# Block outputs of a fused two-layer kernel: four full-array products, or eight products of 64 rows and 64 columns

## The chip, the core and the metric

The kernel runs on one core of a Trainium2 chip. A core has TensorE (matrix products, results in PSUM), VectorE (DVE), ScalarE (ACT), GpSimd (POOL) and SyncE (SP, which issues the transfers here). PSUM has eight banks of 2 KiB for each of 128 partitions; a bank holds 512 f32 numbers. The metric is the time of one execution on the device in microseconds (us), the median of several runs. Lower is better.

## What is computed

x has the shape (4, 64, 256, 256), f32. Two layers follow each other, each a residual around a group norm.

```
x = x + L0(group_norm(x))     # 1x1 convolutions, a 3x3 depthwise one, an 8x8 FFT filter, a GELU gate
x = x + L1(group_norm(x))     # two state-space blocks over the image, one by rows, one by columns
...
fx = layer_norm(seq)                       # over the 64 channels
h = s5_scan(fx)                            # forward and backward scan, 64 complex states
x = gelu(h) + fx
fx2 = layer_norm(x)                        # over the 64 channels
y = fx2 @ ff_enc.T @ ff_dec.T + fx2
...
out = concat(y_rows, y_columns) @ fusion_w.T + fusion_b
```

The change lies in the last three lines: layer 1, from gelu(h) + fx to its share of the fused output. ff_enc, ff_dec, the `+ fx2`, the centring of the second layer norm and fusion_w are multiplied together ahead of time into one matrix of 64 by 64 for each of the two directions.

## The kernel before

Layer 0 runs first, strip by strip of eight rows over the four images, and writes its result to a scratch tensor in DRAM (`x1d`). Then each image goes through layer 1 in a first pass (`pass_a`), a scan (`scan`) and a second pass (`pass_b`). The first pass normalises, stores the normalised strips (`fxd`) and makes one summary for each short segment of a sequence; the scan runs over the summaries; the second pass fills in the states within the segments and makes the output.

Partitions hold 64 channels twice: the lower 64 partitions are one row of the image, the upper 64 another row, with the same channels.

The second pass works in units. A unit is one strip of 16 rows (s, 16 of them) in one direction (d=1 by columns, d=0 by rows); the list `order` takes d=1, then d=0 of each strip, so 32 units an image and 128 in all. A unit has four blocks of 512 columns, taken in the order `blocks = (1, 2, 0, 3)`. Its steps, each a function in `pass_b`:

- `states` (L1378): products into PSUM tile `pst` (two banks, one buffer), then one VectorE operation for each step (tiles `stm`, `sto`). For d=1 these are products over 128 rows with 512 columns; for d=0 they are pairs of 64 rows and 256 columns, one half in each of the two banks.
- `filt` (L1409): products into `ph` (one bank, two buffers). For d=1 these use the whole array, 512 and 256 columns; for d=0 they write halves of 64 output partitions, two beside each other. GELU on ScalarE, an addition on GpSimd and a square on ScalarE follow, and give `xr` (the block's 128x512 result) and `sq`.
- `sums` (L1449) and `rstd_of` (L1463): sums over channels into `pv` (one bank), four transposes back into `pv`, and the reciprocal standard deviation `r` of every position, once a unit.
- `outputs` (L1478): for one block, four products with 128 columns of `xr` as the stationary operand (`lhsT`) and the matrix `wb[d][:, NB[d]]` as the moving one, into `px`. That matrix is 128 by 128 with the 64x64 matrix twice on its diagonal and zeros elsewhere. VectorE multiplies the result by `r` into `y` (positions on partitions).
- `emit` (L1488): four transposes of `y` into another `px`, which VectorE adds to the strip (`acc`, tile `strip`); after the last block of a d=0 unit the strip is stored.

`px` is one bank with three buffers, shared by `outputs` and `emit`. With `pst` 2, `ph` 2, `px` 3 and `pv` 1 all eight banks are taken.

The order on every engine is the order of the program: `mm` and `vec` keep it. The loop over n runs four quarters for each unit. In a quarter come, one after the other: `states` of the unit ahead (first part), the steps of earlier units that are due in the first half, `filt` (first part), `states` (second part), `filt` (second part), and the steps due in the second half. The table `behind` says what is due:

```
for i, k in enumerate(blocks):
    behind[7 + i, 1] = [(outputs, k)]
    behind[8 + i, 0] = [(emit, k)]
behind[4, 1] = [(sums,)]
behind[5, 1] = [(rstd_of,)]
```

The first number is 4 times the delay in units plus the quarter, the second is the half. So every quarter ends with the `outputs` of one block; in the first quarter `sums` of the unit before comes right behind them, in the second `rstd_of`. The next quarter's `states` follows, and then the block's `emit`. After the last unit of an image three more rounds of the loop hold only these late steps.

A product over f32 appears in the trace as two weight loads and two matmuls. In the profile, the form `64*128 64x256` means 64 rows by 128 columns of the array and a moving operand of 64 by 256; `128*64` means all rows and 64 columns of the array.

Of the kernel before, what the change touches and what calls it, by code (L numbers as in the profile page):

```python
# [16 lines left out]
C = 64  # L17
HID = 170
S = 256
P = 128  # L20
# [90 lines left out]
def tile_kernel(ctx: ExitStack, tc: tile.TileContext, x, cst, w0, winp, wdwp, w1, out):  # L111
# [3 lines left out]
    def new(pool, shape, tag, bufs=None, dt=F32):  # L115
        return pool.tile(shape, dt, tag=tag, name=tag, **({} if bufs is None else {"bufs": bufs}))
# [77 lines left out]
    with ExitStack() as l0:  # L194
# [17 lines left out]
        for h in range(2):  # L212
            p = slice(h * C, (h + 1) * C)
# [39 lines left out]
        with tc.tile_pool(name="pssp", bufs=1, space=PSUM) as pp:  # L253
            ps = new(pp, [P, 512], "sp")
# [6 lines left out]
        NA, NB = (16, 8), (32, 25)  # L261
# [16 lines left out]
        with ExitStack() as l1w:  # L278
# [35 lines left out]
            def tmp(n=2, dt=F32):  # L314
                n_tmp[0] += 1
                return new(sp, [P, n], f"tmp{n_tmp[0]}", None, dt)
# [49 lines left out]
            def mul(a, b):  # L366
                o = tmp()
                TT(o, a, b, ALU.mult)
                return o
# [28 lines left out]
            t = mul(lim, lim)  # L398
            TT(den, den, t, ALU.add)
            vec.reciprocal(di, den)  # L400
            qr, qi, u, t = tmp(), tmp(), mul(lbi, lim), mul(nr, lre)
            TT(qr, t, u, ALU.add)
            u, t = mul(nr, lim), mul(lbi, lre)
# [142 lines left out]
            u, t, r, i = mul(ur, ur), mul(ui, ui), tmp(), tmp()  # L546
# [9 lines left out]
            n = 1  # L556
# [26 lines left out]
            for d in range(2):  # L583
                w = lambda name, d=d: wts[d][:, W1_AT[name][0] : W1_AT[name][0] + W1_AT[name][1]]
                ps = new(pw, [P, 512], "pw")
# [9 lines left out]
            for d in range(2):  # L595
                ps = new(pw, [P, 512], "pw")
# [7 lines left out]
                for h in range(2):  # L604
                    p = slice(h * C, (h + 1) * C)
                    TS(wos[d][p, p], mts[d][p, 0, :], par(d, "g2")[p], None, ALU.mult)
            burst[1]()
            for d in range(2):
                mm(
                    psb[:, 0:1], lhsT=mts[d][0:C].rearrange("p h c -> p (h c)"), rhs=par(d, "b2")[0:C],  # L610
                    start=(d == 0), stop=(d == 1),
                )
                ps = new(pw, [P, 512], "pw")
# [14 lines left out]
        pp = l0.enter_context(tc.tile_pool(name="ps0", bufs=2, space=PSUM))  # L628
# [321 lines left out]
        for b in range(nb):  # L950
            if b + 1 < nb:
                nxt_stats = new(wk, [P, 2 * NS0, 6], "stats1")
            for s in range(NS0):
                n = b * NS0 + s
# [97 lines left out]
    def rows_of(s):  # L1052

        for k in range(2):
            for hi in range(2):
                yield slice(k * C, (k + 1) * C), slice(4 * hi, 4 * hi + 4), s * R1 + 8 * hi + (k ^ hi)
# [22 lines left out]
    with tc.tile_pool(name="psn", bufs=2, space=PSUM) as pn:  # L1079
        for b in range(nb):  # L1080
# [4 lines left out]
            ps = new(pn, [P, 512], "pn")  # L1085
# [227 lines left out]
    def pass_b(b):  # L1313

        with ExitStack() as es:
# [4 lines left out]
            wb = [new(wp, [P, NB[d] + 1, P], f"wb{d}") for d in range(2)]  # L1320
# [20 lines left out]
            pp = es.enter_context(tc.tile_pool(name="psb", bufs=2, space=PSUM))  # L1341
# [7 lines left out]
            def mm(*args, **kw):  # L1349
                tc.keep_in_program_order(nc.tensor.matmul(*args, **kw))  # L1350
# [127 lines left out]
            def outputs(u, i):  # L1478


                ps, xr = new(pp, [P, 512], "px", 3), u.pop(("xr", i))
                for k in range(4):
                    mm(ps[:, k * P : (k + 1) * P], lhsT=xr[:, k * P : (k + 1) * P], rhs=wb[u["d"]][:, NB[u["d"]]], start=True, stop=True)
                y = u["y", i] = new(wk, [P, 512], "y")
                yv, pv = (t.rearrange("p (k h c) -> p k h c", k=4, h=2) for t in (y, ps))
                vec.tensor_tensor(yv, pv, u["r"][:, :, i].unsqueeze(3).to_broadcast([P, 4, 2, C]), ALU.mult)

            def emit(u, i):  # L1488
                y, acc = u.pop(("y", i)), u["acc"]
                ps = new(pp, [P, 512], "px", 3)  # L1490
                for k in range(4):
                    tc.keep_in_program_order(nc.tensor.transpose(ps[:, k * P : (k + 1) * P], y[:, k * P : (k + 1) * P], ident))  # L1492
                if u["d"] == 1:
                    o = acc[:, 2 * i : 2 * i + 2].rearrange("p r (g q) -> p r q g", q=16)
                    vec.tensor_tensor(o, ps.rearrange("p (r q g) -> p r q g", r=2, q=16), o, ALU.add)
                    return
                o = acc.rearrange("p r (g q) -> p q (r g)", q=16)[:, 4 * i : 4 * i + 4]
                vec.scalar_tensor_tensor(o, ps.rearrange("p (q t) -> p q t", q=4), bias, o, ALU.add, ALU.add)
                if i == blocks[-1]:
                    for h, r, row in rows_of(u["s"]):  # L1500
                        nc.sync.dma_start(out=out[b, :, row : row + 7 : 2, :], in_=acc[h, r])
# [3 lines left out]
            blocks = (1, 2, 0, 3)  # L1505
            behind = {}
# [3 lines that stand above are left out]
# [7 lines left out]
            for n in range(len(order) + 3):  # L1517
                if n < len(order):
                    s, d = order[n]
# [110 lines left out]
```

## Time and profile before

| | |
|---|---|
| median of 3 runs | 8972.83 us (8968.28 to 8975.56) |
| the profiled execution | 8968.82 us |
| its span, first to last instruction | 8967.0 us |
| granted TensorE clock over the span | 0.986 |
| TensorE busy, weight loads busy | 8424.2 us, 5727.6 us |
| VectorE busy | 7092.5 us |
| outputs: matmuls into px from wb, xr | 4096, 569.5 us busy |
| outputs: y on VectorE | 512, 354.1 us busy, 692 ns each |
| emit: transposes into px | 2048, 325.6 us busy |
| emit: additions to the strip on VectorE | 256 of 1025 ns, 256 of 1117 ns |

PE is TensorE's matmul row, PEld its weight loads, which can run beside matmuls. A group line gives the source line, engine, operation, tiles (out<-in), form, count, then busy us, mean ns of one, and the idle time of the engine before them with what ended it. A timeline line gives the start in us, the duration in us, the engine, the operation and how many instructions are merged in it. The ends of matmul rows are modelled; their starts are not.

### The profile page before, as it was taken

The page shows a single profiled execution, that of the slowest core. Times are in us where ns is not written, and L with a number is a line of the kernel's source. Part 1 is how long each engine was busy: PE and PEld are TensorE (multiplying, and loading weights), DVE is VectorE, ACT ScalarE, POOL GpSimd, SP SyncE. Part 2 cuts the span into 40 slices and gives each one's busy share as a digit, 9 for nine tenths or more (in the row PEclk, how much of TensorE's full clock was granted, in tenths as well). Part 3 has the DMA queues.
Part 4 walks back from the last instruction along what each step waited for, and adds up shares of the span by engine and source line. Part 5 has one row for each costly group of instructions (what it writes and reads, how often), then busy time and mean ns, then how long its engine had stood idle before and what let it go on. Part 6 is the DMA issues. An engine that isn't in the chain of part 4 may idle for free. (4 is left out here: it accounts for less than half of the span.)

```text
span 8967.0 us, 184750 instructions
## 1 busy us (share of the span) xinstructions
PE 8424.2 (94%) x79478; PEld 5727.6 (64%) x79478; DVE 7092.5 (79%) x8837; ACT 3404.5 (38%) x5094; POOL 2408.0 (27%) x1282
## 2 busy tenths in 40 slices
PE   3999999999999999998899988999988999889999
PEld 2666666666666666665466655566654666555666
DVE  7999999999999999995767756777656677567776
ACT  3444444444444444436322245222263222452222
POOL 3000000000000000005644446444356444464443
PEclk9999999999999999999999999999999999999999
DMA  7444344444444333325233345133352333451332
GB/s 176 101 104 102 95 108 100 105 101 97 102 104 103 83 87 83 87 63 175 103 81 81 90 120 178 49 84 82 82 169 103 81 81 90 120 178 49 84 82 70
DMA packets 655264, 904.19 MB, mean 101 GB/s; under 512 B 43120, under 2 KB 584816, under 8 KB 618864
## 3 DMA queue, kind: packets, MB, share of 16 engines
q1 hardware_dynamic: 654448, 892.37, 37.3%
q8 instruction: 627, 10.27, 0.5%
q14 instruction: 189, 1.55, 0.1%
HBM read 583.86 MB, written 275.05 MB: 96 GB/s over the span
## 5 line engine op out<-in xcount | busy, mean ns | idle before, releaser
L207 PE MATMUL m<-v,sw 64*128 64x256 f32 (+1 forms) x8192 | 1541.8, 392 | 1.6 <-DVE v L303 1.1
L207 PEld LDWEIGHTS m<-v,sw 64*128 64x128 f32 (+1 forms) x8192 | 1121.7, 188 | 505.1 <-issue 359.2
L303 DVE SCALAR_TENSOR_TENSOR acc<-xat,taps,acc 128x1024 f32<-128x1024 f32 x1024 | 1311.5, 1281 | 16.6 <-ACT acc L164 2.9
L1445 POOL TENSOR_TENSOR xr<-xr,fx 128x512 f32<-128x512 f32 x512 | 650.6, 1271 | 1863.8 <-ACT xr L1444 1378.9
L1350 PE MATMUL pst<-fx,wb 64*128 64x256 f32 (+1 forms) x4992 | 1017.3, 438 | 37.5 <-DVE stm L303 18.3
L694 POOL MEMSET at<- 64x256 f32 x4 | 1.2, 308 | 3525.4 <-DVE v L303 3525.4
L1350 PEld LDWEIGHTS pst<-fx,wb 64*128 64x128 f32 (+1 forms) x4992 | 508.4, 187 | 372.1 <-issue 244.4
L1475 POOL TENSOR_TENSOR rs<-ve,mhalf 128x32 f32<-128x32 f32 x128 | 695.3, 5432 | 99.2 <-DVE ve L303 99.2
L303 DVE SCALAR_TENSOR_TENSOR stm<-stm,step,pst 128x512 f32<-128x512 f32 x640 | 478.6, 748 | 232.9 <-PE pst L1350 219.3
L1446 ACT ACTIVATE sq<-xr 128x512 f32<-128x512 f32 x512 | 322.8, 631 | 872.5 <-POOL xr L1445 872.5
L207 PEld LDWEIGHTS m<-ct,hw 128*64 128x64 f32 x16384 | 509.7, 138 | 117.7 <-issue 117.7
L303 DVE SCALAR_TENSOR_TENSOR sto<-sto,step,pst 128x512 f32<-128x512 f32 x512 | 382.9, 748 | 242.7 <-PE pst L1350 228.8
L1350 PE MATMUL px<-wb,xr 128*128 128x128 f32 x4096 | 569.5, 282 | 0.0
L303 DVE TENSOR_TENSOR z<-xc,pr 128x512 f32<-128x512 f32 x256 | 264.8, 1036 | 385.2 <-PE pr L1106 382.2
L1350 PEld LDWEIGHTS px<-wb,xr 128*128 128x128 f32 x4096 | 519.8, 193 | 54.2 <-issue 41.8
L303 DVE TENSOR_TENSOR y<-px,rs 128x512 f32<-128x512 f32 x512 | 354.1, 692 | 229.2 <-PE px L1350 220.1
L1350 PE MATMUL ph<-sto,wb 128*64 128x128 f32 (+1 forms) x5120 | 528.0, 299 | 0.0
L207 PE MATMUL m<-ct,hw 128*64 128x64 f32 x16384 | 527.3, 223 | 0.0
L1350 PE MATMUL ph<-stm,wb 128*64 128x128 f32 (+1 forms) x5120 | 525.0, 299 | 0.0
L1350 PEld LDWEIGHTS ph<-stm,wb 128*64 128x64 f32 (+1 forms) x5120 | 409.0, 147 | 144.5 <-issue 128.0
L164 POOL TENSOR_TENSOR rs<-ve,mhalf 128x32 f32<-128x32 f32 x64 | 347.7, 5433 | 566.0 <-DVE ve L303 554.3
L1350 PEld LDWEIGHTS ph<-sto,wb 128*64 128x64 f32 (+1 forms) x5120 | 405.0, 147 | 143.0 <-issue 129.8
(316 smaller groups left out, 15615.0 us busy)
## 6 DMA issues: line engine op xcount, KB each, us to landing
strip<-x1d SPq DMA_DIRECT2D x512, 256.0 KB, 7.4
fx<-fxd SPq DMA_DIRECT2D x128, 1024.0 KB, 6.9
at<-in_x_dram SPq DMA_DIRECT2D x248, 320.0 KB, 4.5
sx<-in_x_dram SPq DMA_DIRECT2D x256, 256.0 KB, 4.0
pr<-in_x_dram SPq DMA_DIRECT2D x256, 256.0 KB, 4.2
er<-in_x_dram SPq DMA_DIRECT2D x256, 256.0 KB, 4.1
x1d<-x SPq DMA_DIRECT2D x256, 256.0 KB, 4.0
fxd<-fv SPq DMA_DIRECT2D x64, 1024.0 KB, 4.7
```

The lines of the kernel that those rows point to most:

```text
L164: return lambda *args, **kw: tc.keep_in_program_order(getattr(self.engine, name)(*args, **kw))
L207: tc.keep_in_program_order(nc.tensor.matmul(*args, **kw))
L303: tc.keep_in_program_order(getattr(nc.vector, name)(*args, **kw))
L694: nc.gpsimd.memset(at[C:P, 4, 1 : S + 1], 0.0)
L1350: tc.keep_in_program_order(nc.tensor.matmul(*args, **kw))
L1445: nc.gpsimd.tensor_tensor(xr, xr, fx, ALU.add)
L1446: nc.scalar.activation(sq, xr, AF.Square)
L1475: nc.gpsimd.tensor_tensor(r, ve.rearrange("p n c -> p (n c)"), mhalf, ALU.pow)
```

## The change

`outputs` no longer multiplies 128 rows of `xr` by the 128x128 matrix with its two zero quarters. For each of the four 128-column pieces it makes two products: rows 0 to 63 with the upper left 64x64 of the matrix, and rows 64 to 127 with the lower right one. The stationary operand is 64 rows by 128 columns of `xr`, the moving one 64 rows by 64 columns. The two halves write to different banks of a new PSUM tile `po` of two banks and one buffer. Two successive blocks of a unit share one `po`: the first takes columns 0 to 255 of both banks, the second columns 256 to 511. VectorE's `y` reads both banks, in the order in which it writes. The tile `px` stays for `emit` alone and falls from three buffers to one, so that all eight banks are taken as before.

```
             def outputs(u, i):
-                ps, xr = new(pp, [P, 512], "px", 3), u.pop(("xr", i))
+                d, xr, n = u["d"], u.pop(("xr", i)), blocks.index(i) % 2
+                if n == 0:
+                    u["po"] = new(pp, [P, 2, 512], "po", 1)
+                ps = u["po"][:, :, n * 256 : (n + 1) * 256]
                 for k in range(4):
-                    mm(ps[:, k * P : (k + 1) * P], lhsT=xr[:, k * P : (k + 1) * P], rhs=wb[u["d"]][:, NB[u["d"]]], start=True, stop=True)
+                    for h in range(2):
+                        p = slice(h * C, (h + 1) * C)
+                        mm(
+                            ps[:, h, k * C : (k + 1) * C], lhsT=xr[p, k * P : (k + 1) * P], rhs=wb[d][p, NB[d], p],
+                            start=True, stop=True,
+                        )
                 y = u["y", i] = new(wk, [P, 512], "y")
-                yv, pv = (t.rearrange("p (k h c) -> p k h c", k=4, h=2) for t in (y, ps))
+                yv, pv = y.rearrange("p (k h c) -> p k h c", k=4, h=2), ps.rearrange("p h (k c) -> p k h c", k=4)
                 vec.tensor_tensor(yv, pv, u["r"][:, :, i].unsqueeze(3).to_broadcast([P, 4, 2, C]), ALU.mult)
 
             def emit(u, i):
                 y, acc = u.pop(("y", i)), u["acc"]
-                ps = new(pp, [P, 512], "px", 3)
+                ps = new(pp, [P, 512], "px", 1)
```

The order of the steps on every engine stays as it was, apart from the eight products in the place of four.

## The prediction

> **What bounds the kernel now.** I read the page's busy shares and slices first, then the windows of one undisturbed stretch of the second pass, then the groups with their shapes kept apart, and last the timeline of TensorE around the step that is changed.
>
> ```profile
> PE 8424.2 (94%) x79478; PEld 5727.6 (64%) x79478; DVE 7092.5 (79%) x8837; ACT 3404.5 (38%) x5094; POOL 2408.0 (27%) x1282
> PE   3999999999999999998899988999988999889999
> PEclk9999999999999999999999999999999999999999
> ```
>
> ```profile
> core 0: us, PE busy (x) PEld busy (x) DVE busy (x) ACT busy (x) POOL busy (x), PEclk, DMA share, GB/s
> 5680.00:6240.00 560.00, 556.15 (x4204) 384.67 (x4203) 385.93 (x561) 146.17 (x272) 231.70 (x112) 1.00 0.30 80
> ```
>
> In 560 us of the second pass TensorE is busy for 556 at the full clock (1.00); VectorE, next, has 386, that is 69%. The second pass is TensorE's alone: whatever TensorE's queue gets longer or shorter by is the time. Busy is no peak, however: the changed products can be limited by streaming columns, by loading weights, or by a change of the array's tiling. The groups (busy us, mean ns of one, idle before):
>
> ```profile
> L1350 PE MATMUL px<-wb,xr 128*128 128x128 f32 x4096 | 569.5, 282 | 0.0
> L1350 PEld LDWEIGHTS px<-wb,xr 128*128 128x128 f32 x4096 | 519.8, 193 | 54.2 <-issue 41.8
> L1492 PEld LDWEIGHTS px<-ct,y 128*128 128x128 f32 x2048 | 234.5, 141 | 250.5 <-issue 146.2 <-DVE y L303 84.4 <-DVE ve L303 19.9
> L1102 PEld LDWEIGHTS ps<-sd,wa 64*128 64x128 f32 x4096 | 238.3, 188 | 21.6 <-issue 21.6
> L207 PEld LDWEIGHTS m<-ct,hw 128*64 128x64 f32 x16384 | 509.7, 138 | 117.7 <-issue 117.7
> ```
>
> To be seen: a load of 64 rows by 128 columns lasts 188 ns, one of 128 by 128 lasts 193, one of 128 by 64 lasts 138. Columns make a load long; rows do not. And f32 costs two instructions for a product: 4096 for the 512 x 4 of the outputs. Now the timeline:
>
> ```profile
> 5812.25 0.28 PE L1350 MATMUL ph<-sto,wb 128*64 128x128 f32 x2
> 5812.45 0.97 PEld L1350 LDWEIGHTS px<-wb,xr 128*128 128x128 f32 x8 [0.17 <-issue]
> 5813.34 0.30 PEld L1350 LDWEIGHTS pst<-fx,wb 128*128 128x128 f32 x2
> ...
> 5829.24 0.38 PE L1350 MATMUL ph<-stm,wb 128*128 128x256 f32 x1
> 5829.55 0.19 PEld L1350 LDWEIGHTS pst<-fx,wb 64*128 64x128 f32 x2 [0.33 <-issue]
> ...
> 5839.50 0.69 DVE L303 TENSOR_TENSOR y<-px,rs 128x512 f32<-128x512 f32 x1 [0.41 <-PE px L1350]
> 5840.45 0.42 PEld L1492 LDWEIGHTS px<-ct,y 128*128 128x128 f32 x4 [0.33 <-DVE y L303]
> 5840.84 0.30 PEld L1350 LDWEIGHTS ph<-fx,wb 128*128 128x128 f32 x2
> ```
>
> ```profile
> 4092.34 0.30 PEld L1102 LDWEIGHTS ps<-sd,wa 64*128 64x128 f32 x4
> 4093.91 0.20 PEld L1102 LDWEIGHTS ps<-sd,wa 64*128 64x128 f32 x2
> 4094.02 0.27 PE L1102 MATMUL ps<-sd,wa 64*128 64x128 f32 x1
> 4094.22 0.19 PEld L1102 LDWEIGHTS pc<-strip,cenr 128*128 128x128 f32 x1
> ```
>
> Pitch now: eight loads of the outputs start in 5813.34 - 5812.45 = 0.89 us, so one instruction each 0.111 us. The transposes into px have the same 128 columns to stream but a shorter load (141 ns); their pitch is (5840.84 - 5840.45 - 0.06 of exposed load) / 3 = 0.109. The outputs are thus already at the limit of their loads.
>
> Pitch in the changed form: the first pass's row summaries (ps) have the form that the outputs get, two halves of 64 rows, two banks, the same 64x128 loads, only with 128 streamed columns in place of 64. From 4092.34 to 4093.91 lie 14 pairs: 0.112 us for a pair.
>
> A change of tiling: the last product of ph starts at 5812.25 and streams 0.109; the next load starts at 5812.45, 0.09 after that, and its 0.107 us stand open (the first product's row, which takes the open load in, lasts 0.38, the median row 0.275; in one tiling the load lies under the product before). So 0.20 us a change. The same from 5829.24 (256 columns, 0.216): 5829.55, again 0.09. And out of the 64-row form (4094.02 to 4094.22): again 0.09. Ahead of transposes, whose load stands open for about 0.06 (0.33 for the first row, 0.27 for the others), it is 0.15.
>
> **The change, part by part.**
> (1) Four products become eight, 8 instructions become 16, two beside each other. What is streamed falls from 128 to 64 columns; each pair still needs a load of 128 columns of xr. Here a rule is to be weighed. The Trainium skill, TensorEngine Tiling (Array Packing), section Theoretical Speedup, gives up to 2x for a dimension of at most 64. By it the eight pairs would take half of 0.89 us, 0.45 us less for a block, 228 us over 512 blocks. The row says 0.112 a pair with the same loads, as long as one instruction now: nothing. I take the row. (The skill's TensorE: Matmul & The Clock Gate, section LDWEIGHTS, speaks the same way, against the change: a load costs its columns, not its rows.) What is left of the gain is the last product, which ends 0.05 us sooner (64-column products, m<-ct,hw, keep a pitch of 0.0585: 64 loads in 1.95 us of the timeline, 31 pitches and one load). It counts only where a change of tiling waits for that end.
>
> (2) Changes of tiling. The same page, section Key Properties, says that a change of mode drains TensorE, without a price; the trace's price is the 0.20 above. Eight blocks, one pair of units, have these neighbours in program order (A = 128x128, R = 64 rows, C = 64 columns, V = 32 columns; the block itself was A, is R now):
> - A, block, V (block beside the sums, filter of d=1): one change more, +0.20 - 0.05 = +0.15
> - A, block, A (beside the transposes of the sums): two more, +0.20 + 0.15 - 0.05 = +0.30
> - A, block, R, twice: the change is only moved from behind the block to before it: 0
> - C, block, V: two before, two after: -0.05
> - C, block, A (transposes): +0.15 - 0.05 = +0.10
> - C, block, A (states of d=1), twice: +0.20 - 0.05 = +0.15 each
> Sum +0.80 us a pair of units. 60 such pairs (480 blocks) make 48 us; the other 32 blocks lie in the four tails, where outputs and transposes follow each other, at about +0.15: 5 us. Together +53 us.
>
> (3) y on VectorE reads two banks with the same 512 elements. No row shows such a read for y; between 0.69 us as now and 0.75, as the 128x512 operations of two tensors and a scalar take. I take 0.69. VectorE is not the bound. But the transposes wait for y: after the A, block, R blocks, y ends at 5839.50 + 0.69 = 5840.19 and the load starts at 5840.45; the trace's closest waits have 0.05 between, so about 0.2 is spare. The moved change of tiling takes about 0.15 of it. It just fits: 0. Were y longer by 0.06, 120 blocks might lose 0.05 each, 6 us.
>
> (4) Buffers: px falls from 3 banks to 1, po takes the two. A transpose into px waits for VectorE's addition of the block before, a quarter of a unit (some 6 us) earlier; po's half was read one pair of blocks before, and within a pair the first half's read ends before the transposes between. Cost 0, covered by those 6 us; without cover it would be the addition, 1.0 us a block. Order of instructions on VectorE, ScalarE, GpSimd and the DMA queues does not change.
>
> The profiled execution took 8968.82 us (span 8967.0 and 1.8 around it), 4.0 below the median of 8972.83 and within the runs shown. 8968.82 + 53 = 9021.8; at the median 9026.
>
> **The rivals.**
> - Faster: the load of 64 rows costs half, or hides. The pair's pitch would fall to the 0.0585 of 64 columns: 8 x (0.112 - 0.0585) = 0.43 us a block, 219 us for all, less the 53: 8972.8 + 53 - 219 = 8807. It decides as soon as a pair takes under 0.099 (53 / 512 / 8 = 0.013 less). For it: 64 streamed columns with 128 loaded ones are nowhere in this trace. Against: 188 ns beside 193; and at the head of the ps stretch the first loads start at 4092.24, the second at 4092.34, 0.1 later with nothing to stream yet. 5%.
> - No change: changes of tiling overlap with waits, or the pitch comes near 0.099, and the gain eats the price: 8973. Against: TensorE waits for nothing in that stretch. 7%.
> - A wait in place of the spare: y arrives later (two-bank read, one px buffer) and the transposes in the 120 tight blocks lose 0.2 us: 24 us more, 9050. For it: the spare falls to some 0.05. 11%.
> - The halves do not run beside each other: 16 loads at 0.112, 0.9 us a block, 460 us, 9485. Against: ps and pst are written the same way and pair. 2%.
> - My forecast: 75%.
>
> **The numbers.** Low end: a pitch of 0.109 in place of 0.112 gives 8 x 0.003 x 512 = 12 us back, a change at 0.18 in place of 0.20 on six net changes x 60 another 7, and tails that cost nothing 5: 9002. High end: y's 6, and changes at 0.215 with the half's lag behind its partner another 9, 9041; then on to the rival of a wait, 9050, with some of these on top: 9056. A measurement of this kernel can tell about 0.2% (18 us) from no change: under 8955 is faster, over 8991 slower. The forecast, the wait and the unpaired halves (88%) are slower, the second rival (7%) is within, the first (5%) faster; left out of the range are the faster one, no change and the unpaired halves, and a few hundredths at its ends.
>
> **What would show it.** Loads and products of po of 64*128, 8192 each; the pitch of a pair near 0.112; the load before the outputs at 0.3 after the last product of a d=1 filter, not prefetched; that of the states behind them prefetched where both are R; px's transposes with hardly more idle time on y. A pitch of 0.06 would prove me wrong at (1); changes that cost far from 0.2, at (2); a new wait of px on y or strip, at (3) or (4).

## The result, and the profile after

The changed kernel takes 9021.47 us in the median of 4 runs (9015.13 to 9027.24), the kernel before 8974.19 beside it: ratio 1.0055, 95% interval 1.0042 to 1.0068. Five more runs of the changed kernel on another occasion gave 9025.57 and 1.0059 (1.0045 to 1.0073). The change makes the kernel slower by half a per cent, some 50 us. The profiled execution took 9015.13 us, its span 9013.4 (8967.0 before).

The same 560 us of the second pass (length, busy us of TensorE, its loads, VectorE, ScalarE and GpSimd, then the granted clock, DMA share and GB/s):

```profile
5680.00:6240.00 560.00, 552.87 (x4760) 373.15 (x4759) 380.11 (x549) 142.21 (x263) 224.98 (x109) 1.00 0.29 76
```

In this stretch TensorE is idle for 7.1 us, where it was 3.8. That is no new wait: the second pass of this image starts 10 us later than before (at 5676.4, not 5666.6), and two waits of 1.6 us for VectorE at its start, which lay ahead of the stretch before, now lie in it. That shift, together with the slower pairs of units, is also why fewer VectorE operations (549 for 561) fall into it. The groups of the changed steps:

```profile
L1350 PE MATMUL po<-wb,xr 64*128 64x64 f32 x8192 | 578.1, 282 | 0.0
L1350 PEld LDWEIGHTS po<-wb,xr 64*128 64x128 f32 x8192 | 507.0, 191 | 127.9 <-issue 127.9
L303 DVE TENSOR_TENSOR y<-po,rs 128x512 f32<-128x512 f32 x512 | 353.7, 691 | 265.0 <-PE po L1350 255.8 <-POOL rs L1475 8.6
```

Twice as many products of half the columns are busy for 578.1 us in place of 569.5. A load of 64 rows lasts 191 ns, one of 128 rows lasted 193. The loads' idle time went from 54.2 us to 127.9, none of it a wait for another engine ("issue"): the loads no longer follow on a load in the same tiling. The read of two banks by y costs nothing (691 ns, 692 before). In the timeline, a block between a d=0 filter and the states of d=1, and one between a d=1 filter and the states of d=0:

```profile
5827.48 0.97 PEld L1350 LDWEIGHTS po<-wb,xr 64*128 64x128 f32 x16 [0.17 <-issue]
5828.52 0.30 PEld L1350 LDWEIGHTS pst<-fx,wb 128*128 128x128 f32 x2
...
5804.39 0.97 PEld L1350 LDWEIGHTS po<-wb,xr 64*128 64x128 f32 x16 [0.33 <-issue]
5805.28 0.74 PEld L1350 LDWEIGHTS pst<-fx,wb 64*128 64x128 f32 x8
5805.62 0.69 DVE L303 TENSOR_TENSOR y<-po,rs 128x512 f32<-128x512 f32 x1 [0.64 <-PE po L1350]
5806.36 0.20 PEld L1501 LDWEIGHTS px<-ct,y 128*128 128x128 f32 x2 [0.34 <-DVE y L303]
```

Eight pairs of loads take the 0.97 us that eight single loads took. In the second block the next loads, of the same tiling, start 5805.28 - 5804.39 = 0.89 after the first, so 0.111 a pair, as one instruction before. In the first block the tiling changes behind the block too, and the next load starts only after 1.04, where it was 0.89. The last two lines are the transposes' wait for y, which ends at 5805.62 + 0.69 = 5806.31; their load follows 0.05 later.

The steady measure for all that follows is the time from the transposes of the sums (pv from ct, sums) of one d=0 filter's unit to those two units later, so one pair of units, eight blocks. Two lines of the kernel before, then two of the changed one:

```profile
5858.08 0.27 PE L1468 MATMUL pv<-ct,sums 128*128 128x128 f32 x1
5908.27 0.27 PE L1468 MATMUL pv<-ct,sums 128*128 128x128 f32 x1
...
5868.72 0.33 PE L1468 MATMUL pv<-ct,sums 128*128 128x128 f32 x1
5919.69 0.33 PE L1468 MATMUL pv<-ct,sums 128*128 128x128 f32 x1
```

50.19 before and 50.97 after, so +0.78 a pair of units. Over the whole traces the medians of this distance are 50.19 and 50.98, so +0.79, and 104 of 116 lie within 0.02 of them; 60 pairs make 47 us.

### The profile page after: what moved, and what is told of

It reads as the page before. It is cut to its first block, busy times and chain, and to the rows that moved or that the text cites. A ratio compares the mean times of both kernels' runs of the same rounds, so it can differ in the third digit from the quotient of the medians.

```text
span 9013.4 us, 192942 instructions
## 1 busy us (share of the span) xinstructions
PE 8477.2 (94%) x83574; PEld 5719.1 (63%) x83574; DVE 7098.8 (79%) x8837; ACT 3404.0 (38%) x5094; POOL 2408.5 (27%) x1282
## 5 line engine op out<-in xcount | busy, mean ns | idle before, releaser
L1350 PEld LDWEIGHTS po<-wb,xr 64*128 64x128 f32 x8192 | 507.0, 191 | 127.9 <-issue 127.9
L1350 PE MATMUL po<-wb,xr 64*128 64x64 f32 x8192 | 578.1, 282 | 0.0
L303 DVE TENSOR_TENSOR y<-po,rs 128x512 f32<-128x512 f32 x512 | 353.7, 691 | 265.0 <-PE po L1350 255.8
```

What stands on the lines that cost most here:

```text
L303: tc.keep_in_program_order(getattr(nc.vector, name)(*args, **kw))
```

## Experiments

The theory: (L) the 128 columns of a load set the pitch of the outputs, whatever is streamed and however many rows are loaded, and each change of tiling costs about 0.2 us. Rivals: (W) a wait, from the single px or from y's read of two banks; (I) the doubled number of instructions.

| run | what it is | median us | ratio (95%) | pair of units us |
|---|---|---|---|---|
| before | | 8974.19 | 1 | 50.19 |
| after | | 9021.47 | 1.0055 (1.0042 to 1.0068) | 50.97 |
| narrow | 4 products on the whole array, 64 columns streamed | 8954.44 | 0.9979 (0.9971 to 0.9987) | 49.88 |
| quads | 16 products of 64x64, four side by side | 8844.58 | 0.9866 (0.9851 to 0.9882) | 48.16 |
| buffers | the change's buffers only | 8967.64 | 0.9999 (0.9991 to 1.0007) | 50.19 |
| placed | the change, outputs moved beside 64-row states | 8991.17 | 1.0027 (1.0017 to 1.0037) | 50.48 |
| after_again | the change once more | 9025.57 | 1.0059 (1.0045 to 1.0073) | 50.98 |
| columns | halves by columns, not by rows | 8985.90 | 1.0019 (1.0013 to 1.0026) | 50.55 |
| quads_placed | quads and placed together | 8849.03 | 0.9865 (0.9852 to 0.9879) | 48.17 |

The kernel before ran beside each group, with medians of 8974.19, 8969.91 (first four experiments) and 8969.93 (last three). The code below is in short form (names shortened, lines that only follow from the change left out).

**narrow: is it the load or the stream?** Against the kernel before:

```
-    mm(ps[:, k*P : (k+1)*P], lhsT=xr[:, k*P : (k+1)*P], rhs=wb[d][:, NB[d]])
+    mm(ps[:, k*P : k*P + C], lhsT=xr[:, k*P : (k+1)*P], rhs=wb[d][:, NB[d], 0:C])
```

This kernel leaves out half of the products' columns; VectorE's y reads the half that is there twice, so its work stays.

> The kernel before with its four products a block on the whole array, but with only the first 64 columns of the matrix as the moving operand: 64 columns streamed instead of 128, the same 128x128 loads, no change of tiling, no extra instruction. The upper 64 channels of the output then get the lower half's numbers, since their columns are not computed. If the load of 128 columns sets the pitch (0.112 us an instruction whatever is streamed), only the last product of a block ends 0.05 us sooner, and only in front of a change of tiling (4 of 8 blocks): 12 us less than before, about 8962. If the streamed columns set it, 8 x (0.112 - 0.0585) x 512 = 219 us less: about 8755.

Measured: 8954.44, 0.9979. Timeline of one block, loads:

```profile
5810.15 0.97 PEld L1350 LDWEIGHTS px<-wb,xr 128*128 128x128 f32 x8 [0.17 <-issue]
5811.03 0.30 PEld L1350 LDWEIGHTS pst<-fx,wb 128*128 128x128 f32 x2
```

Half of what is streamed is gone, and eight loads still take 5811.03 - 5810.15 = 0.88 us. The stream was not the limit in the kernel before; the load was. The 19 us that did go are 0.31 a pair of units, where I had expected 0.20: by the starts of the products, the shorter last product counts in six of eight blocks, not four. Ahead of the transposes of the sums, which are in the same tiling, it gives 0.045 us (0.053 ahead of a change), ahead of the states of d=1 nothing.

**quads: shorter loads.** Against the changed kernel:

```
     p = slice(h * C, (h + 1) * C)
-    mm(ps[:, h, k*C : (k+1)*C], lhsT=xr[p, k*P : (k+1)*P], rhs=wb[d][p, NB[d], p])
+    for g in range(2):
+        q = k * P + g * C
+        mm(ps[g*C : (g+1)*C, h, k*C : (k+1)*C], lhsT=xr[p, q : q + C], rhs=wb[d][p, NB[d], p])
```

> The changed kernel with each product of 64 rows and 128 loaded columns split again, into two that load 64 columns each: four 64x64 parts of the array beside each other, 16 products a block (32 instructions), the same 64 columns streamed, in the same two banks. If the columns of a load set the pitch, a step of four takes about 0.0585 us in place of 0.112, and a change of tiling opens 0.05 us of load less; against that, two of the eight blocks of a pair of units get a change behind them that they share with the states now: about 3.0 us a pair of units less than the changed kernel, 60 pairs and the tails: 190 us less than 9021, about 8830. If instructions are the limit (twice as many) the pitch stays at 0.112 or grows: 9021 to 9060 or more. In between (0.08): about 8910.

Measured: 8844.58. It beats the kernel before by 1.3%. A block of quads:

```profile
5924.55 0.56 PEld L1350 LDWEIGHTS po<-wb,xr 64*64 64x64 f32 x32 [0.17 <-issue]
5925.18 0.30 PEld L1350 LDWEIGHTS pst<-fx,wb 128*128 128x128 f32 x2
```

Four times the loads of the kernel before take 0.56 us in place of 0.97, and the next step's load starts after 0.63 in place of 1.04 in the changed kernel: 0.41 less, where 8 x (0.112 - 0.0585) = 0.43 had been worked out. So twice as many instructions again cost nothing, which rules out (I). A pair of units fell by 2.81, 0.2 less than the 3.0 expected. That remainder is a new wait, seen where 64-row states follow a block:

```profile
5947.55 0.73 PEld L1350 LDWEIGHTS pst<-fx,wb 64*128 64x128 f32 x8 [0.33 <-issue]
5949.68 0.56 PEld L1350 LDWEIGHTS po<-wb,xr 64*64 64x64 f32 x32 [0.33 <-issue]
5950.38 0.76 PEld L1350 LDWEIGHTS pst<-fx,wb 64*128 64x128 f32 x8
...
5948.74 1.53 DVE L303 SCALAR_TENSOR_TENSOR stm<-stm,step,pst 128x512 f32<-128x512 f32 x2 [0.79 <-PE pst L1350]
```

pst has one buffer. Its products start at 5947.55, VectorE is done with them at 5948.74 + 1.53 = 5950.27, and the next products into pst start at 5950.38, 0.70 after the block's first load and not 0.63. The round trip of 2.83 us was hidden behind the longer outputs; twice in eight blocks it now shows, 0.08 each. The count agrees: behind all 120 such blocks of quads the states' load starts 0.12 us after VectorE's read of pst, the least distance that 64-row states have in any of these traces; behind those of the changed kernel it is 0.30.

**buffers: is it a wait?** Against the kernel before: outputs take `new(pp, [P, 512], "po", 2)`, emit `new(pp, [P, 512], "px", 1)`.

> The kernel before with only the buffers of the change: outputs in two banks of their own, emit's px with one buffer. Four products on the whole array as before. If loads and changes of tiling explain the result, no difference from before: 8974, within 6 us. If the single buffer of px is behind the loss (a wait of the transposes for the addition to the strip), some or all of the 47 us appear: up to 9021.

Measured: 0.9999 (0.9991 to 1.0007), and 5910.37 - 5860.18 = 50.19 for a pair of units, as before. The single px costs nothing. Here po is two tiles of one bank, not the one tile of two banks that the change has; for that one and for y's read, (W) rests on the changed kernel's own profile: no load of po waits for VectorE there, and y takes 691 ns. Of (W), under 1 us is left, in the transposes that wait for y (point 3 below).

**placed: take changes of tiling away.** The changed kernel, with the outputs called behind the states, and the second half of the late steps without outputs in those quarters:

```
     states(units[m], group, 1)
+    if m < len(order) and units[m]["d"] == 0:
+        late(1, True)      # the outputs that are due in this half
```

> The changed kernel with its outputs moved ahead of the second half of the filter, right behind the states of a d=0 unit (64 rows too), in the four quarters of a pair of units that have such states in their second half. Nothing else is changed. If a change of tiling costs 0.2 us, this takes away the one before and the one behind the block beside the transposes of the sums (0.35 us), the one before the block beside the sums (0.2) and 0.05 at the other two: 0.65 us a pair of units, 39 us for 60: about 8982, near the kernel before. If the loss comes from the doubled instructions or from y's read of two banks, it stays: about 9021.

Measured: 8991.17, 1.0027; a pair of units 50.48, so 0.49 less than the changed kernel, where 0.65 was expected. The stretch with the transposes of the sums:

```profile
5885.03 0.73 PEld L1350 LDWEIGHTS pst<-fx,wb 64*128 64x128 f32 x8 [0.33 <-issue]
5885.79 1.08 PEld L1350 LDWEIGHTS po<-wb,xr 64*128 64x128 f32 x16
5886.93 0.73 PEld L1350 LDWEIGHTS ph<-stm,wb 128*128 128x128 f32 x4
5887.69 0.58 PEld L1468 LDWEIGHTS pv<-ct,sums 128*128 128x128 f32 x4
...
5891.94 0.76 PEld L1350 LDWEIGHTS pst<-fx,wb 64*128 64x128 f32 x8 [0.46 <-issue]
```

The outputs' loads now start right behind the states' last, with no idle time before them, and the transposes follow the filter without a change. The same eight pairs, less idle time around them: that is the price of the changes. What is missing of the gain stands in the last line: those states start 0.13 later than a change alone lets them (0.46 for 0.33). VectorE, which has to release pst first, says why:

```profile
5889.03 1.15 DVE L303 TENSOR_TENSOR ve<-ve,m 128x32 f32<-128x32 f32 x1
...
5891.07 0.75 DVE L303 SCALAR_TENSOR_TENSOR stm<-stm,step,pst 128x512 f32<-128x512 f32 x1
...
5888.84 1.28 POOL L1445 TENSOR_TENSOR xr<-xr,fx 128x512 f32<-128x512 f32 x1 [7.96 <-ACT xr L1444]
```

The small operation on ve, 0.19 us in the changed kernel, lasts 1.15 here and ends at 5890.18, just behind GpSimd's addition (5890.12), into which it has been moved. VectorE's operations on pst follow behind it without a pause, up to the release at 5891.82; the states' load starts 0.12 later, the least distance. No run takes the operation on ve out of the addition again, so its share of the missing 0.16 us is read from the rows and not tested.

**after_again: how much is chance?**

> The changed kernel once more, with more rounds. Loads and changes of tiling as worked out: 47.6 us for the 60 pairs of units and about 5 for the four tails, so 1.0059 of the kernel before, 9022 or so. The first profile had 15 us less in the first pass, which the change does not touch; if that is chance, the first pass comes back to some 1245 us and the ratio to 1.005 to 1.007. If the change does make the first pass shorter, it stays at 1235 and the ratio at 1.005.

Measured: 9025.57, 1.0059; the first pass, from its first product of a strip to the scan and summed over the four images, 1243 us. It was 1250 before, 1235 in the first profile of the changed kernel, 1242 in buffers. Over the nine profiles here the first pass, which no run edits, takes 1235 to 1250 us, and the same kernel gave both 1235 and 1243. The 15 us that the first profile had less are within that scatter: chance, as far as one profile of each kernel can tell.

**columns: the other half.** Against the kernel before, in the place of each of the four products:

```
+    for g in range(2):
+        q = k * P + g * C
+        mm(ps[g*C : (g+1)*C, k*P : (k+1)*P], lhsT=xr[:, q : q + C], rhs=wb[d][:, NB[d]])
```

> The kernel before with its outputs cut the other way: all 128 rows, but 64 columns of xr to a load, two products beside each other on the column halves, the whole 128 columns of the matrix streamed; px and its three buffers as before. The load is halved, what is streamed is not, so a pair stays at 0.109 us (0.112 before), and the block now has the tiling of the d=0 filter in front of it. By the price of a change (0.2 us, 0.15 where a short load follows) a pair of units gains 0.22, 0.07 and twice 0.02 in the d=0 filter's quarters and loses 0.13, 0.28 and twice 0.13 in the d=1 filter's: 0.33 us more, 20 us for 60, with the tails 23: about 8993. If the halved load counts by itself, as the halved rows did not, 8 x (0.112 - 0.0585) x 512 = 219 us less, about 8770. If neither loads nor changes matter: 8970.

Measured: 8985.90, 1.0019; a pair of units 50.55, so +0.36 where 0.33 was expected. Behind a d=0 filter, whose tiling the block shares:

```profile
5809.11 1.73 PEld L1350 LDWEIGHTS ph<-sto,wb 128*64 128x64 f32 x32 [0.17 <-issue]
5810.81 0.91 PEld L1350 LDWEIGHTS px<-wb,xr 128*64 128x64 f32 x16
5811.88 0.30 PEld L1350 LDWEIGHTS pst<-fx,wb 128*128 128x128 f32 x2 [0.17 <-issue]
```

No idle time before px, 0.17 behind it: the change of tiling has moved from before the block to behind it. The pairs' loads start 0.109 us apart (median), though each loads 64 columns: now the 128 streamed columns set the pitch. So (L) holds only while no more columns are streamed than loaded. Halving the load alone gains nothing, as halving the rows or the stream alone did not.

**quads_placed.**

> Both together: four 64x64 products beside each other, and the outputs moved right behind the states of a d=0 unit in the four quarters that have them. Against the four-part kernel alone (8845) one change fewer, about 0.25 us, at the block beside the transposes, and 0.08 at the two blocks that had 64-row states behind them: 0.4 us a pair of units, 24 us for 60, less some 8 us in which states wait for VectorE, as in the moved kernel before: about 8829, the fastest of all. If moving the outputs gains nothing with short loads: 8845.

Measured: 8849.03, 0.9865, where 8829 was expected; a pair of units 48.17, as in quads alone, so moving the outputs gains nothing here. The changes of tiling are fewer, but the states wait for pst:

```profile
5941.37 0.76 PEld L1350 LDWEIGHTS pst<-fx,wb 64*128 64x128 f32 x8 [0.46 <-issue]
...
5944.22 0.76 PEld L1350 LDWEIGHTS pst<-fx,wb 64*128 64x128 f32 x8 [0.40 <-PE ph L1350]
```

The 0.40 would be 0.33 for a change alone. In the group of the small operation on ve the mean is 1.08 us here, 0.64 in quads, 0.63 in placed, 0.19 in the changed kernel. And the round trip of pst from 5941.37 to 5944.22, 2.85 us, is that of quads (2.83). In this trace 256 loads for 64-row states start at the least distance of 0.12 us behind VectorE's read, 196 in quads, so 60 more, one a pair of units: TensorE no longer sets this stretch alone, so a change of tiling saved there is given back as a wait.

## Why the prediction was right, and where its sizes were off

Predicted 9026 (9002 to 9056) and slower; measured 9021.47, and 9025.57 in the second group.

1. *The pitch.* 0.111 us for a pair in place of one instruction, as taken from the row summaries. narrow shows that it is the load also on the whole array, columns that 128 streamed columns hold it at 0.109 when the load is halved, quads that it falls to 0.058 when both are. The rule of a factor of two for a dimension of 64, which I put aside for the row, holds neither for rows alone (after) nor for columns alone (columns); with both halved (quads), on four parts of 64x64, the eight steps take about half.
2. *The changes of tiling.* The trace gives, from the start of the last product before the block to the start of the fourth behind it (the row of the first takes in its load where that stands open, so a later one is compared), these medians against the kernel before: +0.147 (A, block, V), +0.298 (A, block, A), +0.002 (A, block, R), -0.050 (C, block, V), +0.100 (C, block, transposes), +0.145 (C, block, states): each within 0.005 of what was worked out, and 0.79 in the sum for 0.80. placed took some away and got time back, columns exchanged them.
3. *y and its spare.* y costs the same. The spare of the transposes shrank as said: from the end of y to their load 0.23 us before and 0.08 after (medians of the 120 blocks), with 0.05 as the least. At half of the 120 blocks it is at that least, and the load starts 0.014 us later behind the block's first product than at the others (1.970 for 1.956): 0.8 us in all. It just fitted, as the prediction said, with nothing over: the rival of a wait was near.
4. *The buffers.* Nothing (buffers).
5. *The tails.* Put at 5 us. In the two profiles they are 102.0 us before and 114.4 after, 12 more; but part of that goes with the clock. The stretches from the last filter to the last transposes of an image, before:

```profile
5232.50:5260.00 27.50, 19.67 (x121) 15.32 (x118) 14.33 (x21) 2.37 (x4) 8.41 (x4) 0.80 0.36 81
6467.10:6491.20 24.10, 15.87 (x122) 11.83 (x116) 14.05 (x21) 2.37 (x4) 8.33 (x4) 1.00 0.44 92
```

and after:

```profile
5244.50:5273.10 28.60, 21.24 (x185) 15.70 (x182) 14.59 (x21) 2.37 (x4) 8.48 (x4) 0.77 0.36 78
```

Behind each stretch stand its length and the busy times; the granted clock is the third figure from the end (0.80, 1.00, 0.77). At a like clock a tail is 27.5 before and 28.6 after, 1.1 more, 4.4 for four: the 5 was right. Three of the four tails of the kernel before had more clock in that profile (1.00, 0.93, 0.93), which makes the other 8 us. Whether the change has a part in that stays open: all eight tails in the two profiles of the changed kernel have a low clock (0.73 to 0.78, 28.6 us each), but so have the four of buffers (0.80 to 0.82), with the products of the kernel before.

So the profiles' 46 us are 47 of the pairs of units, 12 of the tails (of which 8 by the clock), 15 less in the first pass, and 2 more in layer 0 and the scans. The 47 are what the prediction worked out. That the first profile's total came so near to it as well is in part luck: the first pass and the clock of the tails, which it left out, moved in opposite directions.

## What to carry to other kernels

Before cutting a product into parts of the array, look at which of its two operands sets the pitch: if the start-to-start time equals that of the load's columns, as 0.111 us for 128 columns did here, halving rows or streamed columns gains nothing, and the cut has to halve the columns of the load as well as what is streamed. Then count the neighbours in program order: a cut is paid for in changes of tiling, 0.15 to 0.2 us each here, and can be free beside steps that have the same tiling. After a gain, look at the single-buffered tile next in line: here the round trip of pst, 2.83 us, became the next bound.

## What the runs showed of the hardware that was not expected

- Thirty-two loads and thirty-two products of a quads block start within 0.63 us, the four loads of a step 7 ns apart; TensorE's issue was no limit at that rate.
- VectorE's 128x32 operation of two tensors in SBUF lasts 1.15 us in place of 0.19 when GpSimd's 1.28 us addition of two SBUF tensors is running, and ends with it. The Trainium skill, SBUF — State Buffer, section Who interferes with whom, says that a VectorE instruction with two SBUF inputs contends with a GpSimd instruction that reads SBUF, and that the order of issue decides which of them blocks. The rows agree: in placed the addition starts 0.19 us ahead of the operation on ve, while in the changed kernel it is over (5895.12) when that operation starts (5895.25). It turned a reordering on TensorE into a wait.
- In the tails, where TensorE waits for y, the granted clock was between 0.80 and 1.00 in the same piece of program, within one execution of the kernel before; that piece took from 24.1 to 27.5 us.
